# Seven-product output projections and two batches per attention output in a two-layer graph attention kernel

## The chip, the cores and the metric

The kernel runs on one core of one Trainium2 chip. The metric is device time in microseconds (us), from the first to the last instruction of the core. The engines are named as in the profile: PE is TensorE, PEld its weight loads, DVE is VectorE, ACT is ScalarE, POOL is GpSimd and SP is SyncE, which here issues all DMAs. Each engine works through its own queue in order, and waits on semaphores where it needs another's result.

## The reference

The input is `x` (128 batches, 128 nodes, 512 features, float32) with a boolean adjacency mask `adj` (128, 128, 128). Two layers follow, each `x = layernorm(x + attention(x, adj))`.

```python
# layer 0: 4 heads of 64
q, k, v = split_heads(x @ Wq), split_heads(x @ Wk), split_heads(x @ Wv)
attn = softmax(where(adj, q @ k.T * 64**-0.5, -max))
x = layernorm(x + (attn @ v) @ Wo + bo)
# layer 1: 8 heads of 64, norm in front, every node also sees itself
h = (x - mu) * rsqrt(var + 1e-5) * gamma + beta
q, k, v = split(h @ w_qkv.T)
attn = softmax(where(adj | eye, q @ k.T * 64**-0.5, -1e9))
x = layernorm(x + (attn @ v) @ w_out.T + b_out)
```

## The kernel before, in words

The batches are taken in 64 groups of two (G = 2). A software pipeline runs over steps s = 0 to 66 (`step`, L531). The order of the instructions on every engine is the order in which the Python code issues them, written out by hand under `manual_schedule` (L48). A step works on several groups at once: the layer-0 input products of group s, layer-0 attention of group s-1, layer-1 q and k products of group s-2, v products and layer-1 attention of group s-3. Within a step there are two halves, k = 2s and k = 2s+1, one for each batch of a group; `members(k)` (L381) names the layers and groups that take part.

- Input products: `product_0` (L337) for layer 0, `product` (L275) for layer 1. Both multiply in the Strassen-Winograd form: the two operands are cut into 2 x 2 blocks (batch by half of the contraction, half of the contraction by half of the output), and seven products of half size stand for eight. `sums` (L257) makes the four sums of the left blocks on POOL, `weight_sums` and `weight_sums_0` (L160, L175) those of the weights, once, on DVE. `INTO` (L272) says which PSUM bank takes each product and whether it starts or adds: 1, 6, 7 and 4 share bank "a", 5 and 3 bank "f", 2 has its own. After each product ACT or DVE takes the running value out, and the next product into the same bank waits for that.
- `scores` (L386): per head one product of q and k; then POOL fills a tile with the masked value (L410), DVE copies the unmasked scores over it (L412) and takes the row maximum (L415). For layer 1 the mask is first joined with the unit matrix (L407). The exponentials (`exps`, L421) run on ACT, head by head, and also give the row sums. `normalised` (L427) takes reciprocals on DVE and multiplies on POOL.
- `blocks` (L436) and `probs_arrive` (L454): DVE transposes 32 x 32 blocks, SP stores the result to memory and fetches it back with the blocks exchanged, which completes the transpose.
- `attend` (L458): values times probabilities for one batch k of each layer, then an ACT copy to SBUF (L474).
- `addend` (L476): the residual plus bias, on POOL; for layer 1 an ACT scaling first.
- `residual` (L487): the output product of one batch, one matmul of 128 x 512 for each 128 rows of the contraction (two for layer 0, four for layer 1, L493), then on DVE the addition of the residual (L499), the statistics (L501, L503), and on POOL the reciprocal roots (L506 to L517).
- `norms` (L522): subtract and multiply on DVE; called by `flush` (L56), which runs what `residual` put off. Layer 1's result is stored from there (L528), one batch at a time.
- `turn`, `arrive`, `in_order`, `finish` (L208, L219, L235, L245): the transpose of a layer's input: 32 x 32 blocks on DVE, a store and a fetch, then an ACT copy (layer 0) or ACT scaling with gamma and beta (layer 1), and `sums`.

The eight PSUM banks are split into five for the pool `ps_mm` and one each for "a", "f" and "a0"; layer 0's and layer 1's products share "f". The setup work, 12 row blocks of `w_qkv` and 4 of `w_out` transposed on PE, is spread over steps 0 and 1, a piece at a time (`p` in `step`, L532).

Of the kernel before, what the change touches and what calls it, by code (L numbers as in the profile page):

```python
# [27 lines left out]
def kernel(ctx: ExitStack, tc: tile.TileContext, x, adj, wq, wk, wv, wo, bo,  # L28
# [13 lines left out]
    four = ctx.enter_context(tc.tile_pool(name="four", bufs=4))  # L42
    dram = ctx.enter_context(tc.tile_pool(name="dram", bufs=2, space=bass.MemoryType.DRAM))
    ps_mm = ctx.enter_context(tc.tile_pool(name="ps_mm", bufs=5, space=PSUM))
# [9 lines left out]
    later, waiting = [], []  # L54

    def flush():  # L56
        while later:
            later.pop(0)()

    def exponentials(left=0):  # L60
        while len(waiting) > left:
            waiting.pop(0)()


    X, M = {}, {}

    def load(g):
        if g >= NG:
            return
        X[g] = four.tile([P, G, E], F32, tag="x", name=f"x_{g}")  # L70
        M[g] = four.tile([P, G, N], U8, tag="m", bufs=6, name=f"m_{g}")
        nc.sync.dma_start(X[g], x[g * G:(g + 1) * G].rearrange("b n e -> n b e"))
        nc.sync.dma_start(M[g], adj[g * G:(g + 1) * G].rearrange("b i j -> i b j"))
# [8 lines left out]
    mhalf = const.tile([P, 2], F32, name="mhalf")  # L82
# [6 lines left out]
    for i, w in enumerate((wq, wk, wv)):  # L89
        for h in range(2):  # L90
            nc.sync.dma_start(w0[:, :, h, i, :], w[:, h * HF:(h + 1) * HF].rearrange("(c p) f -> p c f", p=P))

    nc.scalar.activation(w0[:, :, :, 0, :], w0[:, :, :, 0, :], AF.Copy, scale=SCALE)
# [14 lines left out]

    spare = []
    for tag, n in (("qk1", 4), ("v1", 2), ("xT1", 2), ("xs1", 2)):  # L110
        rows_n = one.tile([P, n, E], F32, tag=tag, name=f"raw_{tag}")
        spare.extend(rows_n[:, i] for i in range(n))

    def load_transposed(dst, src, name, scaled=0):
        rows, cols = src.shape
        raws = []
        for r in range(rows // P):
            if not spare:
                raw = three.tile([P, cols], F32, tag="h", bufs=7, name=f"{name}_{r}")
            else:  # L120
                raw = spare.pop(0)
            nc.sync.dma_start(raw, src[r * P:(r + 1) * P, :])
            raws.append(raw)
# [36 lines left out]
    def weight_sums():  # L160
        for w, ws in ((w1qk, wsqk), (w1v, wsv)):
            for c in range(KH):
                if w is w1qk:
                    b11, b12 = w[:, c, :, 0], w[:, c, :, 1]
                    b21, b22 = w[:, KH + c, :, 0], w[:, KH + c, :, 1]
                else:
                    b11, b12 = w[:, c, 0], w[:, c, 1]
                    b21, b22 = w[:, KH + c, 0], w[:, KH + c, 1]
                t2, t3, t4 = ws[:, 0, c], ws[:, 1, c], ws[:, 2, c]
                nc.vector.tensor_sub(t3, b22, b12)  # L170
                nc.vector.tensor_sub(b12, b12, b11)
                nc.vector.tensor_sub(t2, b22, b12)
                nc.vector.tensor_sub(t4, b21, t2)

    def weight_sums_0():  # L175
        b11, b12, b21, b22 = (w0[:, c:c + KH, h].rearrange("p c t f -> p c (t f)")
                              for c in (0, KH) for h in range(2))
        t2, t3, t4 = (ws0[:, i].rearrange("p c t f -> p c (t f)") for i in range(3))
        nc.vector.tensor_sub(t3, b22, b12)
        nc.vector.tensor_sub(b12, b12, b11)  # L180
        nc.vector.tensor_sub(t2, b22, b12)
        nc.vector.tensor_sub(t4, b21, t2)

    weight_sums_0()
# [3 lines left out]
    setup.append(weight_sums)  # L188

    WO = (wo0, wo1)  # L190
    RATIO, H, XT, QK, V, QKV = {}, {}, {}, {}, {}, {}
# [14 lines left out]
    TURNED, SCR, RAW = {}, {}, {}  # L206

    def turn(l, g, b):  # L208
        if not 0 <= g < NG:
            return  # L210
        if b == 0:
            TURNED[l] = one.tile([P, 4, G * KC * 32], F32, tag=f"turned{l}", name=f"turned{l}_{g}")
        src = X[g][:, b] if l == 0 else H[g, b]
        nc.vector.transpose(TURNED[l].rearrange("p a (b c i) -> p a b c i", b=G, c=KC)[:, :, b],
                            src.rearrange("p (c a i) -> p a c i", a=4, i=32))
        if b == G - 1:
            SCR[l] = put(TURNED[l], f"scr{l}_{g}")

    def arrive(l, g):  # L219
        if not 0 <= g < NG:  # L220
            return
        RAW[l] = one.tile([P, 4, G, KC, 32], F32, tag=f"raw{l}", name=f"raw{l}_{g}")
        fetch(RAW[l].rearrange("p a b c i -> p a (b c i)"), SCR[l])

    def first_transposed():
        xT = XT[0, 0] = one.tile([P, KC, T], F32, tag="xT0", name="xT0_0")
        for b in range(G):
            pt = mm_tile(f"xt_{b}")
            for c in range(KC):
                nc.tensor.transpose(pt[:, c * N:(c + 1) * N], X[0][:, b, c * P:(c + 1) * P], ident)  # L230
            (nc.scalar.copy, nc.vector.tensor_copy)[b](xT[:, :, b * N:(b + 1) * N],
                                                       pt.rearrange("p (c n) -> p c n", c=KC))
        sums(0, 0)
# [11 lines left out]
    def finish(g):  # L245
# [4 lines left out]
        xT = XT[1, g] = one.tile([P, KC, T], F32, tag="xT1", name=f"xT1_{g}")  # L250
        for c in range(KC):
# [3 lines left out]
        sums(1, g)  # L255

    def sums(l, g):  # L257
        xT = XT[l, g]
        xs = one.tile([P, 4, KH, N], F32, tag=f"xs{l}", name=f"xs{l}_{g}")
        a = xT.rearrange("p (h c) (b n) -> p b h c n", h=2, b=2)  # L260
# [6 lines left out]
        XS[l, g] = xs  # L267
# [69 lines left out]
    def product_0(g, *which):  # L337
# [5 lines left out]
        for i in which:  # L343
# [10 lines left out]
            elif first:  # L354
                tag = {"a": "a0", "f": "f"}[bank]
                ACC[0, bank] = ps_st.tile([P, 512], F32, tag=tag, name=f"{bank}0_{g}")
# [11 lines left out]
            if i in (1, 5, 6):  # L368
                e = one.tile([P, 512], F32, tag=("e5_0" if i == 5 else f"e{i}"), name=f"e0_{i}_{g}")
                EV[0, i] = e[:, :3 * P]  # L370
# [8 lines left out]
    SM, SUM, PT, AT, XB = {}, {}, {}, {}, {}  # L379
# [6 lines left out]
    def scores(k):  # L386
        both = members(k)
        made = []
        for l, g, b in both:
# [11 lines left out]
            made.append(ps)  # L401
        for (l, g, b), ps in zip(both, made):
            K = HEADS[l] // 2
            mask = M[g][:, b, :]
            if l == 1:
                m1 = two.tile([P, N], U8, tag="m1", name=f"m1_{g}_{b}")
                nc.vector.tensor_tensor(m1, mask, eye, op=ALU.max)  # L407
                mask = m1
# [8 lines left out]
            SM[l, g, b], SUM[l, g, b] = sm, total  # L417
            waiting.append(lambda sm=sm, nmax=nmax, total=total, K=K: exps(sm, nmax, total, K))
        exponentials(1)

    def exps(sm, nmax, total, K):  # L421
# [14 lines left out]
    def blocks(k):  # L436
# [6 lines left out]
        t = one.tile([P, 4, sum(HEADS), 32], F32, tag="turned", name=f"turned_{k}")  # L443
        pT = one.tile([P, 4, sum(HEADS), 32], F32, tag="pT", name=f"pT_{k}")
        for l, g, b in both:
            lo, hi = slots[l]
            sm = SM.pop((l, g, b)).rearrange("p s k (q r) -> p q (s k) r", r=32)
            nc.vector.transpose(t[:, :, lo:hi, :], sm)  # L448
            PT[l, g, b] = pT[:, :, lo:hi, :]
        lo, hi = slots[both[0][0]][0], slots[both[-1][0]][1]  # L450
        t, pT = (u[:, :, lo:hi, :].rearrange("p a h i -> p a (h i)") for u in (t, pT))
        SCR["p"] = pT, put(t, f"scrp{hi - lo}_{k}")
# [5 lines left out]
    def attend(k):  # L458
        both = members(k)
        if not both:  # L460
            return
        for l, g, b in both:
            K = HEADS[l] // 2
            pT = PT.pop((l, g, b))
            pm = mm_tile(f"av{l}_{g}_{b}")

            for h in range(HEADS[l]):
                s, kk = h % 2, h // 2
                o = pm[s * D:(s + 1) * D, kk * N:(kk + 1) * N]
                v = QKV[g][:, b, kk, 2, s * D:(s + 1) * D] if l == 0 else V[1, g][:, b, h * D:(h + 1) * D]  # L470
                nc.tensor.matmul(o.rearrange("p (a r) -> p a r", r=32), v, pT[:, :, s * K + kk, :],  # L471
                                 start=True, stop=True)
            AT[l, g, b] = two.tile([P, INNER[l]], F32, tag=f"aT{l}", name=f"aT{l}_{g}_{b}")
            nc.scalar.copy(AT[l, g, b], pm[:, :INNER[l]])  # L474

    def addend(l, k):  # L476

        for _, g, b in [m for m in members(k) if m[0] == l]:
            if l == 0:
                xin = X[g][:, b, :]  # L480
            else:
                xin = H.pop((g, b))
                nc.scalar.activation(xin, xin, AF.Copy, scale=RATIO.pop((g, b)))  # L483
            nc.gpsimd.tensor_tensor(xin, xin, (bias0, bias1)[l], op=ALU.add)  # L484
            XB[l, g, b] = xin

    def residual(l, k):  # L487
        for _, g, b in [m for m in members(k) if m[0] == l]:
            aT = AT.pop((l, g, b))
            nk = INNER[l] // P  # L490
            pm = mm_tile(f"o{l}_{g}_{b}")
            for c in range(nk):
                nc.tensor.matmul(pm, aT[:, c * P:(c + 1) * P], WO[l][:, c, :],  # L493
                                 start=(c == 0), stop=(c == nk - 1))
            if l == 0:
# [134 lines left out]
```

## Time and profile before

| | us |
|---|---|
| median of three runs | 2984.34 |
| lowest, highest | 2983.19, 2987.64 |
| span of the profiled execution | 2982.7 |

| engine | busy us | instructions |
|---|---|---|
| PE | 2920.0 | 22089 |
| PEld | 2402.9 | 22089 |
| DVE | 1854.0 | 3291 |
| ACT | 1334.2 | 4619 |
| POOL | 1567.4 | 2055 |

Weight loads (PEld) overlap matmuls, so their time is not added to PE's. Groups of instructions that the change touches, from the list of groups: their line, count, and mean length of one.

| group | count | mean ns |
|---|---|---|
| L493 output product, 128x512 | 1536 | 600 |
| L499 addition of the residual, 128x512 | 256 | 672 to 692 |
| L524 norm of layer 1, of layer 0 | 128, 128 | 892, 547 |
| L335 addition, v products, 128x256 | 192 | 385 to 415 |
| L266 sums of left blocks, 128x256 | 512 | 726 to 731 |
| L474 attention copy, 128x256, 128x512 | 128, 128 | 357, 580 |
| L407 mask with unit matrix, 128x128 | 128 | 281 |

A mean length counts from the start of an instruction to its end; since matmuls are pipelined, the time that one adds is read from the starts of its neighbours in the timeline. One product of the source is two matmul instructions here.

### The profile page before, as it was taken

How to read it: one execution, taken by the hardware profiler on the slowest of the kernel's cores; microseconds unless marked ns; L12 is line 12 of the kernel's file. 1: busy time of each engine (PE TensorE's matmuls, PEld its weight loads, DVE VectorE, ACT ScalarE, POOL GpSimd, SP SyncE). 2: the span in 40 equal slices, each digit the busy share in tenths (PEclk: the TensorE clock that was granted, in tenths of full speed). 3: DMA queues.
4: the chain of work that ended last, by engine and by line, in shares of the span. 5: the costliest groups of instructions: out<-in, count | busy, mean ns of one | idle time of the engine just before them, and what ended most of it. 6: DMA issues, size and time to landing. Idle time of an engine off the chain costs nothing.

```text
span 2982.7 us, 59421 instructions
## 1 busy us (share of the span) xinstructions
PE 2920.0 (98%) x22089; PEld 2402.9 (81%) x22089; DVE 1854.0 (62%) x3291; ACT 1334.2 (45%) x4619; POOL 1567.4 (53%) x2055
## 2 busy tenths in 40 slices
PE   6899999999999999999999999999999999999997
PEld 5788888888888888888888888888888888888865
DVE  4466666666666666666656666666666666666654
ACT  2344444444444444444544444444444444444442
POOL 2455545545545555555555555455455455455543
PEclk8999999999999999999999999999999999999999
DMA  5454544544544544544544545545445445445332
GB/s 170 123 149 129 150 141 127 161 136 124 165 135 125 165 136 127 160 134 134 156 132 140 150 131 147 146 129 153 141 126 161 137 122 168 133 125 163 118 100 89
DMA packets 249136, 414.42 MB, mean 139 GB/s; under 512 B 41608, under 2 KB 181392, under 8 KB 248848
## 3 DMA queue, kind: packets, MB, share of 16 engines
q1 hardware_dynamic: 248848, 410.62, 46.3%
q8 instruction: 175, 2.87, 0.4%
q14 instruction: 113, 0.93, 0.1%
HBM read 209.72 MB, written 200.80 MB: 138 GB/s over the span
## 4 chain that ended last, share of the span: by engine, by line
PE 96%; DVE 1%; DMA 1%; ACT 1%; issue 0%; POOL 0%; SPq 0%; POOLq 0%; DVEq 0%; ACTq 0%
PE o L493 22%; PE qka L304 15%; PE a L361 12%; PE qkf L304 8%; PE va L304 8%; PE sc L400 6%; PE av L471 6%; PE f L361 6%; PE qkc L304 4%; PE vf L304 4%; PE c L361 3%; PE vc L304 2%; ACT sm L424 1%; DMA scrp<-turned 0%; DMA pT<-scrp 0%
## 5 line engine op out<-in xcount | busy, mean ns | idle before, releaser
L424 ACT ACTIVATE sm<-sm,nmax 128x128 f32<-128x128 f32 x1536 | 595.2, 389 | 618.6 <-DVE nmax L415 604.9
L493 PE MATMUL o<-wo,aT 128*128 128x512 f32 x1536 | 713.2, 600 | 10.0 <-ACT aT L474 10.0
L506 POOL TENSOR_SCALAR ve<-mv 128x1 f32<-128x1 f32 x256 | 57.0, 223 | 1133.0 <-DVE rec L432 798.8
L493 PEld LDWEIGHTS o<-wo,aT 128*128 128x128 f32 x1536 | 278.3, 191 | 269.3 <-issue 246.8
L433 POOL TENSOR_TENSOR sm<-sm,rec 128x512 f32<-128x512 f32 (+1 forms) x256 | 397.0, 1561 | 171.9 <-DVE rec L432 171.9
L412 DVE COPY_PREDICATED sm<-m,sc 128x512 f32<-128x512 uint8 (+1 forms) x512 | 271.0, 581 | 29.1 <-POOL sm L410 7.0
L424 ACT ACTIVATION_READ_ACCUMULATOR sm<-sm,nmax 128x1 f32 x1536 | 288.0, 187 | 0.0
L448 DVE STREAM_TRANSPOSE turned<-sm 128x512 f32<-128x512 f32 (+1 forms) x256 | 246.0, 965 | 45.0 <-POOL sm L433 45.0
L304 PE MATMUL qkf<-xs,w 128*128 128x128 f32 x2048 | 249.9, 275 | 0.1
L304 PE MATMUL qka<-xs,wsqk 128*128 128x128 f32 x2048 | 249.6, 275 | 0.0
L415 DVE TENSOR_REDUCE nmax<-sm 128x4 f32<-128x512 f32 (+1 forms) x256 | 244.0, 953 | 8.8
L304 PEld LDWEIGHTS qkf<-xs,w 128*128 128x128 f32 x2048 | 239.0, 192 | 0.6 <-POOL xs L266 0.4
L304 PEld LDWEIGHTS qka<-xs,wsqk 128*128 128x128 f32 x2048 | 239.0, 192 | 0.0
L524 DVE TENSOR_SCALAR h<-h,mv,rstd 128x512 f32<-128x512 f32 x128 | 70.0, 547 | 265.0 <-POOL rstd L513 265.0
L432 DVE RECIPROCAL rec<-total 128x4 f32<-128x4 f32 (+1 forms) x256 | 44.7, 175 | 296.6 <-ACT sm L424 296.6
L266 POOL TENSOR_TENSOR xs<-xT 128x256 f32<-128x256 f32 x256 | 186.0, 727 | 34.4 <-PE w_qkvt L129 14.5
L410 POOL MEMSET sm<- 128x512 f32 (+1 forms) x256 | 181.1, 735 | 1.4 <-DVE turned L448 1.3
L330 ACT COPY ev<-va 128x256 f32<-128x256 f32 x128 | 47.6, 372 | 298.7 <-PE va L304 298.7
L513 POOL TENSOR_TENSOR rstd<-ve,mhalf 128x2 f32<-128x2 f32 (+1 forms) x256 | 165.9, 648 | 21.3
L330 ACT COPY eqk<-qka 128x512 f32<-128x512 f32 x128 | 75.1, 587 | 214.4 <-PE qka L304 214.4
L484 POOL TENSOR_TENSOR h<-h,bias 128x512 f32<-128x512 f32 x128 | 162.7, 1271 | 7.0 <-ACT h L483 6.9
L484 POOL TENSOR_TENSOR x<-x,bias 128x512 f32<-128x512 f32 x128 | 162.2, 1267 | 0.0
(122 smaller groups left out, 5825.5 us busy)
## 6 DMA issues: line engine op xcount, KB each, us to landing
scrp<-turned SPq DMA_DIRECT2D x124, 768.0 KB, 3.3
pT<-scrp SPq DMA_DIRECT2D x496, 192.0 KB, 4.0
scr<-turned SPq DMA_DIRECT2D x127, 512.0 KB, 2.7
raw<-scr SPq DMA_DIRECT2D x508, 128.0 KB, 3.0
x<-in_x_dram SPq DMA_DIRECT2D x64, 512.0 KB, 4.2
out_dram<-y SPq DMA_DIRECT2D x128, 256.0 KB, 2.0
m<-in_adj_dram SPq DMA_DIRECT2D x64, 32.0 KB, 4.0
scrp<-turned SPq DMA_DIRECT2D x4, 512.0 KB, 3.2
```

The source lines that it names most:

```text
L266: nc.gpsimd.tensor_tensor(o, a0, a1, op=op)
L304: nc.tensor.matmul(o, lhsT, rhs, start=first and n == 0, stop=n == len(todo) - 1, skip_group_check=True)
L361: nc.tensor.matmul(acc[:, t * P:(t + 1) * P], lhsT, rhs, start=first and n == 0, stop=n == len(todo) - 1, skip_group_check=True)
L400: nc.tensor.matmul(ps[h % 2][:, h // 2, :], q_, k_, start=True, stop=True)
L410: nc.gpsimd.memset(sm, (NEG0, NEG1)[l])
L412: nc.vector.copy_predicated(sm[:, s], mask[:, None, :].to_broadcast([P, K, N]), ps[s][:, :K, :])
L415: nc.vector.tensor_reduce(nmax, sm, AX.X, ALU.max, negate=True)
L424: nc.scalar.activation(sm[:, s, k, :], sm[:, s, k, :], AF.Exp, bias=nmax[:, s, k:k + 1], accum_out=total[:, s, k:k + 1])
L433: nc.gpsimd.tensor_tensor(sm, sm, rec[:, :, :, None].to_broadcast([P, 2, K, N]), op=ALU.mult)
L448: nc.vector.transpose(t[:, :, lo:hi, :], sm)
L484: nc.gpsimd.tensor_tensor(xin, xin, (bias0, bias1)[l], op=ALU.add)
L493: nc.tensor.matmul(pm, aT[:, c * P:(c + 1) * P], WO[l][:, c, :], start=(c == 0), stop=(c == nk - 1))
```

## The change

It has these parts, cut to their core in the diff below.

1. The output products are formed in seven products too. `out_product` replaces the matmuls of `residual`: 128 x 256 outputs, one matmul per product for layer 0 and two for layer 1, and after every product DVE adds the bank straight into the residual, which lies in one tile `R[g]` for a group from load to store. `out_sums` makes the left sums on POOL, `weight_sums_out` the weights' sums once.
2. `attend` runs once per step, for both batches of a group; layer 0's two batches share one bank and one ACT copy. It takes the probabilities of the step before.
3. The norms run on ACT (Identity with scale and bias per row) instead of DVE, and layer 1's result is stored for two batches at once. `roots` works on both batches in one instruction, with two more small ones for the shift.
4. The layer-1 mask is made once per group (`with_self`). Masking and exponentials of the two layers are issued at separate places.
5. PSUM: four banks for `ps_mm`, and "a", "f", "a0", "f0". The probabilities' tile has two buffers; the input transposes of the two layers share one.
6. Start: `opening` replaces steps 0 and 1; group 1's input is transposed on PE as group 0's already was. The weights are loaded half by half.
7. End: the last batch's probabilities are transposed on PE (`blocks_direct`) and not through memory. Steps run from 2 to 67.
8. The order in `step` is written anew; `finish` is split in two halves; `load` is one group ahead and first in the step.

```diff
-    ps_mm = ctx.enter_context(tc.tile_pool(name="ps_mm", bufs=5, space=PSUM))
+    ps_mm = ctx.enter_context(tc.tile_pool(name="ps_mm", bufs=4, space=PSUM))
...
-    for i, w in enumerate((wq, wk, wv)):
-        for h in range(2):
+    for h in range(2):
+        for i, w in enumerate((wq, wk, wv)):
...
+    def out_product(l, g, *which):
...
+            for c in range(hk):
+                nc.tensor.matmul(acc, left[:, c], right[:, c], start=first and c == 0, stop=c == hk - 1,
+                                 skip_group_check=True)
+            b, h = {1: (0, 0), 2: (0, 0), 6: (0, 1), 3: (0, 1), 5: (1, 1), 7: (1, 1), 4: (1, 0)}[i]
+            part = R[g][:, b, h * EH:(h + 1) * EH]
+            nc.vector.tensor_add(part, acc, part)
...
+    def attend(s):
+
+        for l, g in ((0, s - 2), (1, s - 4)):
...
+        def norms():
+            for b in range(G):
+                nc.scalar.activation(R[g][:, b], R[g][:, b], AF.Identity, bias=shift[:, b:b + 1],
+                                     scale=root[:, b:b + 1])
+            if l == 1:
+                nc.sync.dma_start(out[g * G:(g + 1) * G].rearrange("b n e -> n b e"), R[g])
...
     def step(s):
...
+        load(s + 1)
+        made = scores(k)
+        masked(made, 0)
+        masked(made, 1)
+        exps(0, k)
+        addend(0, s - 2)
...
+        p("qk", s - 3, 4)
+        product_0(s, 1)
+        attend(s)
+        exps(1, k)
+        out_sums(0, s - 2)
+        product_0(s, 5, 2)
+        out_product(0, s - 2, 1, 5, 2)
+        if s < NG:
+            normalised(k)
+            addend(1, s - 4)
+        out_product(0, s - 2, 6)
+        product_0(s, 6)
+        if s < NG:
+            blocks(k, 0)
+        out_product(0, s - 2, 3, 7)
+        stats(0, s - 2, 0)
+        product_0(s, 3)
+        out_product(0, s - 2, 4)
+        stats(0, s - 2, 1)
+        product_0(s, 7)
+        p("v", s - 3, 1, 5)
...
+        blocks(k, 1)
+        p("v", s - 3, 2)
+        flush()
+        turn(1, s - 2)
+        arrive(1, s - 2)
+        probs_arrive(k)
+        k += 1
+        made = scores(k)
+        masked(made, 0)
+        p("v", s - 3, 6)
+        product_0(s, 4)
+        exps(0, k)
+        masked(made, 1)
+        exps(1, k)
+        p("v", s - 3, 3)
+        out_sums(1, s - 4)
+        flush(latest)
+        out_product(1, s - 4, 1, 5, 2)
+        p("v", s - 3, 7)
+        out_product(1, s - 4, 6, 3)
+        finish(s - 2, 0)
+        p("v", s - 3, 4)
+        normalised(k)
+        turn(0, s + 1)
+        finish(s - 2, 1)
+        out_product(1, s - 4, 7)
...
+        p("qk", s - 2, 1)
+        out_product(1, s - 4, 4)
+        stats(1, s - 4, 1)
+        p("qk", s - 2, 2, 5, 6)
+        in_order(s + 1)
         flush()
+        p("qk", s - 2, 3, 7)
-    for s in range(NG + 3):
+    opening()
+    for s in range(2, NG + 4):
         step(s)
```

## The prediction

> **What bounds the kernel now.** I read the page's busy times first, then busy time by stage, the chain that ended last, the costliest groups, and last the timeline of one step.
>
> ```profile
> PE 2920.0 (98%) x22089; PEld 2402.9 (81%) x22089; DVE 1854.0 (62%) x3291; ACT 1334.2 (45%) x4619; POOL 1567.4 (53%) x2055
> ```
> ```profile
> 0.00:50.00 50.00, 28.67 (x233) 27.28 (x233) 21.53 (x36) 14.25 (x30) 9.72 (x19) 0.99 0.71 226
> 50.00:100.00 50.00, 38.26 (x236) 31.76 (x237) 22.07 (x45) 13.57 (x43) 19.77 (x31) 0.81 0.31 94
> 100.00:150.00 50.00, 46.16 (x365) 39.78 (x364) 28.62 (x52) 21.35 (x78) 24.56 (x31) 0.97 0.40 117
> ...
> 1200.00:1500.00 300.00, 300.00 (x2275) 247.32 (x2274) 189.64 (x338) 137.31 (x473) 166.17 (x219) 1.00 0.49 145
> ...
> 2900.00:2950.00 50.00, 43.73 (x302) 33.83 (x301) 25.53 (x40) 20.27 (x71) 19.46 (x23) 0.97 0.25 80
> 2950.00:2983.00 33.00, 17.23 (x64) 8.82 (x64) 12.00 (x18) 5.85 (x21) 7.07 (x10) 0.86 0.27 87
> ```
> After the bounds of the stretch and its length come the busy times of PE, weight loads, DVE, ACT and POOL, the granted clock and DMA. The middle is one regime, PE busy without a gap; the first 150 us and the last 80 leave PE 37 and 22 us idle, and there its clock also falls. From 300 to 2850 us the list of PE's waits is empty. The chain says the same by line:
>
> ```profile
> PE o L493 22%; PE qka L304 15%; PE a L361 12%; PE qkf L304 8%; PE va L304 8%; PE sc L400 6%; PE av L471 6%; PE f L361 6%; PE qkc L304 4%; PE vf L304 4%; PE c L361 3%; PE vc L304 2%; ACT sm L424 1%; DMA scrp<-turned 0%; DMA pT<-scrp 0%
> ```
> So the time is a sum of matmuls. Scores of the first full step begin at 145.65 us in the chain, those of step 64 at 2854.6: 60 steps of **45.15 us**, a start of 145.65 and a tail of 128.1. PE's timeline of one step (start, length, the line) gives rates:
>
> ```profile
> 1324.56 1.95 PE L304 MATMUL qka<-xT,wsqk 128*128 128x128 f32 x16
> 1326.44 0.66 PE L471 MATMUL av<-pT,qkv 128*64 128x128 f32 x8
> ...
> 1334.84 1.88 PE L493 MATMUL o<-wo,aT 128*128 128x512 f32 x4
> 1336.55 1.03 PE L304 MATMUL va<-w,xT 128*128 128x256 f32 x4
> 1337.42 1.03 PE L304 MATMUL vf<-w,xs 128*128 128x256 f32 x4
> ```
> From start to start: four 512-column instructions take 1.71 us, 0.43 each; four of 256 columns 0.865, 0.216 each. A product in the source is two instructions.
>
> [...] this trace records 191 ns, still under the 216 ns of a 256-column matmul, so loads should stay hidden, as they do in the v rows. [...] qka above takes 1.88 us to av's start, 1.79 where a like product follows; leaving av costs about 0.1 again (1.00 against 0.90). [...] after 5.65 us idle at 44.5 us this trace grants 0.50 from 50 to 60.
>
> **The change part by part, per full step.**
> *Output products, PE.* Removed: 12 products of 512 columns, 24 x 0.43 = 10.32 us. Added: 7 for layer 0 and 14 for layer 1, of 256 columns, 42 x 0.216 = 9.07. **-1.25 us**, all on the path. Lower bound -1.32 (exact 7/8), upper +0.6 if each cost 0.26.
> *Attention of two batches.* One visit to the 64-column mode instead of two: -0.2 (0 to -0.2). [...] **Step: 43.8 us.**
> *DVE.* Added 14 additions 128x256 at 0.41 (v rows, L335): 5.74. Removed 4 of 512 (0.68 each, 2.73), norms 2 x 0.892 + 2 x 0.547 = 2.88, and one of two mask unions, 0.15 net. Sum 0: 28.7 of 43.8 us, beside PE.
> *ACT.* [...] one attention copy of 512 (0.58) for two of 256 (0.36): +3.1, to 23.8 us.
> *POOL.* Sums over attention outputs: 4 x 0.73 for layer 1, 4 x about 0.5 for layer 0 (between a fixed 0.2 and 0.73): +4.9. The small root operations: 5.1 before, between 4 and 6 after. 29.4 us of 43.8. All three hide below PE in throughput.
> *DMA.* Same bytes; one 512 KB store for two of 256, and the loads of x and mask move on SP's queue to the step's start, behind the store of the previous step. They have until the DVE turn some 30 us later; x landed in 4.2 us. Neither is on the path.
>
> **Waits.** Each engine runs in order, so I laid the new order out by hand from the durations above, step start = 0. ACT's exponentials are 0.385 us a head, start to start.
> - PE needs the attention copies at 10.5; ACT has layer 0's at about 7 and POOL its first sum at 7.5. Hidden.
> - Reciprocals stand in DVE's queue before the addition of output product 6. They wait for ACT's eight layer-1 exponentials, which stand behind three attention copies: 8.45 to 11.6. Reciprocals 12.6, addition 13.0, wanted by product 7 at 14.0. Slack 1.0.
> - v1 takes the bank of output product 4 at 17.6; that addition ends at 16.9, behind a 0.9 us stats pair. Slack 0.7.
> - Probabilities of the second batch: stored by 35.2 plus 3.3, fetched by 43 to 44; wanted at 48.5. Slack 4.
> - Layer 1's input is the tight one. Layer-0 stats end at 17.7, roots on POOL behind the 2.5 us bias addition 19.8, norms on ACT 21.1, DVE turns 22.0. Store: in the trace 512 KB land in 2.7 us, but a store at 1341.1 let SP fetch only at 1346.1, 5 us. So the fetch lands at 28.5 (median) to 31.8. ACT then makes half the input (1.1 us) and copies v4, and qk1 wants v4's bank at 31.85. A stall of 0 to 1.5 us. I take 0: in the new order only the 768 KB of probabilities go ahead of that store, and no 768 KB fetch.
> - qk1's later sums follow on POOL at 34.6, wanted at 36.3. Hidden.
>
> **The ends.** Start: before, PE does nothing between 6.7 and 15.25, because q's scaling precedes the transposed copies on ACT and a transpose of weights still in flight precedes the first product. Now product 1 needs only the scaled q and k, v; these land by about 9 to 10, with 1 us of scaling: **-5**. Sixteen weight subtractions (44.2 to 53.2 on DVE) stood before one batch's softmax; both batches of group 0 now pass before them, but group 1's scores wait behind them, with ACT blocked at those exponentials and PE idle some 7 us. The next layer-1 input costs another 9 of PE idle. Adding PE work of about 91 us (setup transposes, two groups' input products, steps 2 and 3) and 12 before the first product, 16 of these waits and 7 of slow clock and smaller waits gives **126** for the start of step 4, against 145.65; bounds 118 and 145.
> Tail: steps 64 and 65 lose their 9.4 us of input products: 36.5 and 36 with 2 us of waits each. The last softmax goes through PE transposes, without the two DMA trips of 4.0 and 3.2 us that stand in the chain at 2949.1 and 2954.5: half a step 8.5, then scores 0.7, mask 2.7, exponentials 3.1, normalise 2.4, transposes and copies 1.6, attention and copies 2.8, sum 0.8, seven products 6.5, stats, roots and norms 3.9, store 2.5, 2 more for hops: 37.5. Together **110**, against 128.1; bounds 102 and 122.
>
> Sum: 126 + 60 x 43.8 + 110 = 2864, against the profile's span of 2982.7; its three runs are 2983.2 to 2987.6, median 1.6 above the span. So **2866**.
>
> **The rivals.**
> 1. *Late layer-1 input.* The wait at qk1 takes the place of the saved matmuls. For it: 5 us for that store in the trace. Against: the store has another neighbour now. At 1.2 us of stall: 2866 + 72 = **2938**.
> 2. *The ends give nothing* (126 and 110 become 145 and 128): **2903**. For it: [...] three long DVE, DMA chains remain in the start.
> 3. *Slower: DVE's queue stops PE.* Mechanism: the reciprocals ahead of output product 6. Slack 1.0 us; every us that ACT's exponentials end later than 11.6 then goes one for one into the step. It decides from 1.0 + 1.35 (the step's gain) + 0.6 (37 us of the ends over 60 steps) = 3 us late. At 3.5 late, 2.5 lost: **3016**. For it: ACT has three copies and, from the last step, norms ahead of them. Against: in the trace these exponentials end 10.4 us after the step's start already.
> 4. *The product doesn't do what it says:* 256-column matmuls with a new load each at 0.26 us instead of 0.216: 42 x 0.26 = 10.9, step +1.8, **2974**. Against: the v rows hold 0.216 with just such loads.
>
> **How the numbers follow.** Forecast 0.58, rival 1 0.17, rival 2 0.14, rival 3 0.08, rival 4 0.03. The forecast's own bounds are about 2835 to 2895; taking in rival 2 and most of rival 1 the range is 2835 to 2940, which leaves out rivals 3 and 4 and the worse part of rival 1, with 3 in 100 below. A measurement tells about 0.2% (6 us) from no change: faster 0.90, within 0.02 (part of rival 4), slower 0.08.
>
> **What would show it.** The output products' chain share falls from 22% to about 20.3% of a shorter span, 9.07 us a step; full steps 43.8 us apart; PE's waits in the middle still empty. Rival 1 shows as PE waiting at a qk start for ACT, rival 3 as PE waiting for DVE at an output product or v1, rival 2 as the first full step after 140 us. I am wrong if steps exceed 44.5 us, or if PE gains a repeated wait.

## The result, and the profile after

The changed kernel took **2955.76 us**, the median of four runs (2953.34 to 2958.32), against 2983.77 before (2981.52 to 2987.64): a ratio of 0.9905, 95% interval 0.9888 to 0.9922. It is faster, by 1% where 4% was forecast, and it lies 16 us above the top of the range. Its profiled execution spans 2956.5 us. The page first: busy times, and the chain by line (the chain is the work that ended last, followed back from the last instruction: at each step to what it had waited for).

```profile
PE 2854.8 (97%) x23257; PEld 2631.1 (89%) x23257; DVE 1818.2 (61%) x3618; ACT 1515.5 (51%) x4811; POOL 1752.2 (59%) x2439
...
PE qka L305 17%; PE a L361 11%; PE oa L397 10%; PE qkf L305 8%; PE va L305 8%; PE sc L425 7%; PE f L361 6%; PE av L529 6%; PE of L397 6%; PE qkc L305 4%; PE vf L305 4%; PE c L361 3%; PE oc L397 3%; ACT xT L252 2%; PE vc L305 2%
```

Output products (oa, of, oc at L397) now hold 10 + 6 + 3 = 19% by the rounded shares, near the 20.3% that was foretold. New at the end of the line is an ACT entry with 2%, where before only PE lines came to more than 1%. PE's busy time fell by 65 us and the span by only 26, so PE now waits. Its list of waits (what waited for what: us in total, times, the longest) gives the place:

```profile
PE qka L305 <- ACT v L333: 40.0, 63, 3.1
PE qka L305 <- ACT xT L252: 9.6, 1, 9.6
PE oa L397 <- ACT aT L534: 7.0, 1, 7.0
```

The first line is the repeated wait, 63 times some 0.63 us on average (0.57 in most steps); the other two stand once each, in the start. Busy time by stage (bounds, length, PE, weight loads, DVE, ACT, POOL, granted clock, DMA):

```profile
50.00:100.00 50.00, 29.60 (x209) 27.39 (x210) 29.68 (x51) 11.84 (x33) 16.05 (x25) 0.80 0.33 96
...
1200.00:1500.00 300.00, 295.97 (x2455) 274.17 (x2454) 186.09 (x375) 158.53 (x503) 183.38 (x252) 1.00 0.50 143
```

The middle, without a gap before, is 4 us short in 300, 0.6 a step. From 50 to 100 us PE does less than before (38.26 then). In PE's timeline step 4's first scores begin at 146.19 and step 64's at 2820.38, which splits the missed time in three:

| | forecast | after |
|---|---|---|
| start, to step 4 | 126 | 146.2 |
| 60 steps | 60 x 43.8 = 2628 | 60 x 44.57 = 2674.2 |
| tail, from step 64 | 110 | 136.1 |
| span | 2864 | 2956.5 |

Half of the miss, 46 us, is the repeated wait with the slower product behind it; the chain shows what it is (start, length, piece).

```profile
1335.00 0.86 PE of L397 x4
1335.86 0.88 PE va L305 x4
1336.74 0.02 issue
1336.77 1.09 ACT xT L252 x2
1337.86 0.27 ACT v L333
1338.12 0.04 issue
1338.16 2.05 PE qka L305 x16
```

ACT does not begin layer 1's new input (`xT`, L252) when the fetch lands but when PE ends the v product of L305. That product is v4 (product 4 of the seven v products) of the *previous* group, and it reads the previous input, from the same tile. ACT's write has to wait for the tile's last reader. In the program `finish(s - 2, 0)` stands ahead of `p("v", s - 3, 4)`, so the copy of v4 (L333) stands in ACT's queue behind the writes that wait for v4. The first qk product (qk1) wants both: its half of the input, and the bank that the copy frees. Nothing but 0.86 us of PE work (output product 7) lies between.

### The profile page after: what moved, and what is told of

It reads as the page before. It is cut to its first block, busy times and chain, and to the rows that moved or that the text cites. A ratio compares the mean times of both kernels' runs of the same rounds, so it can differ in the third digit from the quotient of the medians.

```text
span 2956.5 us, 63007 instructions
## 1 busy us (share of the span) xinstructions
PE 2854.8 (97%) x23257; PEld 2631.1 (89%) x23257; DVE 1818.2 (61%) x3618; ACT 1515.5 (51%) x4811; POOL 1752.2 (59%) x2439
## 4 chain that ended last, share of the span: by engine, by line
PE 93%; ACT 3%; DVE 1%; POOL 1%; issue 1%; DMA 1%; SPq 0%; ACTq 0%; POOLq 0%; DVEq 0%
PE qka L305 17%; PE a L361 11%; PE oa L397 10%; PE qkf L305 8%; PE va L305 8%; PE sc L425 7%; PE f L361 6%; PE av L529 6%; PE of L397 6%; PE qkc L305 4%; PE vf L305 4%; PE c L361 3%; PE oc L397 3%; ACT xT L252 2%; PE vc L305 2%
## 5 line engine op out<-in xcount | busy, mean ns | idle before, releaser
L550 POOL TENSOR_TENSOR r<-r,bias 128x1024 f32<-128x1024 f32 x128 | 303.0, 2367 | 2.9 <-ACT r L549 2.9
L401 DVE TENSOR_TENSOR r<-oa,r 128x256 f32<-128x256 f32 x512 | 215.7, 421 | 80.6 <-PE oa L397 79.8
L305 PE MATMUL qkf<-xs,w 128*128 128x128 f32 x2048 | 249.6, 275 | 0.0
L305 PE MATMUL qka<-xs,wsqk 128*128 128x128 f32 x2048 | 249.6, 275 | 0.0
L305 PEld LDWEIGHTS qka<-xs,wsqk 128*128 128x128 f32 x2048 | 239.0, 192 | 0.0
L305 PEld LDWEIGHTS qkf<-xs,w 128*128 128x128 f32 x2048 | 239.0, 192 | 0.0
L336 DVE TENSOR_TENSOR qk<-qkf,eqk 128x512 f32<-128x512 f32 x64 | 44.3, 692 | 298.8 <-PE qkf L305 275.5
L268 POOL TENSOR_TENSOR so<-aT 128x128 f32<-128x128 f32 (+1 forms) x256 | 151.9, 593 | 113.8 <-ACT aT L534 113.8
L397 PE MATMUL of<-wo,so 128*128 128x256 f32 x768 | 210.3, 383 | 5.3 <-POOL so L268 5.3
L397 PE MATMUL oa<-wso,so 128*128 128x256 f32 x768 | 213.1, 386 | 0.5 <-DVE r L401 0.5
L595 ACT ACTIVATE r<-r,shift,root 128x512 f32<-128x512 f32 x256 | 194.3, 807 | 22.7 <-POOL shift L584 22.7
L252 ACT ACTIVATE xT<-raw,gb 128x256 f32<-128x256 f32 x256 | 139.7, 594 | 117.3 <-PE va L305 111.7
L375 DVE TENSOR_TENSOR qkv<-c,e 128x384 f32<-128x384 f32 x64 | 35.7, 557 | 254.4 <-PE c L361 252.5
L305 PEld LDWEIGHTS qka<-xT,w 128*128 128x128 f32 x1024 | 122.7, 196 | 75.0 <-ACT v L333 65.3
```

The lines of the kernel that those rows point to most:

```text
L268: nc.gpsimd.tensor_tensor(o, a0, a1, op=op)
L305: nc.tensor.matmul(o, lhsT, rhs, start=first and n == 0, stop=n == len(todo) - 1, skip_group_check=True)
L397: nc.tensor.matmul(acc, left[:, c], right[:, c], start=first and c == 0, stop=c == hk - 1, skip_group_check=True)
L401: nc.vector.tensor_add(part, acc, part)
L550: nc.gpsimd.tensor_tensor(R[g], R[g], (bias0, bias1)[l][:, None, :].to_broadcast([P, G, E]), op=ALU.add)
```

## The experiments

Ratios are to runs of the kernel before on the same chip.

**The repeated wait.** Two edits remove it, if the reading is right. One issues v4 earlier and the input later:

```diff
-        out_product(1, s - 4, 6, 3)
-        finish(s - 2, 0)
+        out_product(1, s - 4, 6)
         p("v", s - 3, 4)
+        out_product(1, s - 4, 3)
+        finish(s - 2, 0)
```

> The product v4 is issued one output product earlier, so that 1.7 us of matmuls and not 0.86 lie between it and qk1. Theory W (the write of layer 1's input waits for v4, its buffer's last reader, and v4's copy stands behind it on ACT): PE's 63 waits of 0.57 us at qk1 vanish, full steps 43.8 us instead of 44.57, time about 2908 to 2912. Theory R (the fetched input lands late): the wait stays or moves, time within 5 us of 2956.

Measured: 2909.39 us, ratio 0.9743 [0.9729, 0.9758], with full steps of 43.71 us (43.80 on average over the 60). The other leaves the order alone and gives each half of the input a tile of its own; v4 reads only the second half, so the first needn't wait for it:

```diff
-            XT[1, g] = one.tile([P, KC, T], F32, tag="xT1", name=f"xT1_{g}")
...
+        xT = one.tile([P, KH, T], F32, tag=("xT1", "xT1h")[half], name=f"xT1_{g}_{half}")
```

> Layer 1's transposed input lies in two tiles, one for each half of the contraction; nothing else moves. Theory W: the first half then waits only for earlier readers, ACT starts it when the fetch has landed, some 1.5 us before v4 ends, and the wait at qk1 vanishes: steps about 43.8 us, time about 2910. Theory R: ACT starts it at the same time as now, no change, 2956.

Measured: 2907.74, 0.9741 [0.9726, 0.9755]. Its chain at the same place:

```profile
1360.15 0.86 PE va L311 x4
1361.01 0.86 PE oa L403 x4
1361.88 1.78 PE qka L311 x16
```

ACT is gone from it, PE goes from v4 through output product 7 into the qk product, and that takes 1.78 us instead of 2.05. No transfer was moved, so the wait was for the old tile and not for late data. Wait (0.57 a step) and slow product (0.27) are nearly all of the 0.86 us by which the steps of 43.71 are shorter. In ACT's timeline of this run the first half of the input now starts when the fetch lands, at 1359.83, and is made by 1360.92; the copy of v4 ends at 1361.42. With the old tile out of the way the transfer is next, and by these times it has about half a us to spare.

A third edit exchanges only the two lines, v4 ahead of `finish(s - 2, 0)`, so that the copy stands first in ACT's queue:

```diff
-        finish(s - 2, 0)
         p("v", s - 3, 4)
+        finish(s - 2, 0)
```

> v4 is issued ahead of the first half of layer 1's input, so ACT copies v4 first. If only the copy's place in ACT's queue made the wait (theory C), it shrinks from 0.57 us to about 0, time about 2912. Theory W: qk1 then waits for the input instead, which still starts after v4: no change within 5 us of 2956.

Measured: 2941.42, 0.9854 [0.9839, 0.9868]; both numbers missed. A step takes 44.35. Its chain at the place:

```profile
1329.43 0.61 ACT xT L252
1330.04 0.04 issue
1330.09 0.49 PE qka L305 x2
1330.57 0.00 issue
1330.57 1.83 PE qka L305 x14
```

The copy is out of the way, and the qk product starts after the first of ACT's two input instructions instead of after both and the copy; then it runs 0.49 + 1.83 = 2.32 us instead of 1.78, its second matmul being held until the second instruction ends. The step gains 0.22 us of the 0.86. So the copy's place is a minor part, the reuse of the tile the major.

**Are seven products worth 1.25 us?** Plain products of 512 columns were put back, all else as changed; the left sums on POOL and the sums of the weights are left out.

```diff
+            if i in (1, 3):
+                b, bank = {1: (0, "a"), 3: (1, "f")}[i]
...
+                    nc.tensor.matmul(acc, aT[:, b, c], w[:, c, :], start=c == 0, stop=c == 2 * hk - 1)
+                nc.vector.tensor_add(R[g][:, b], acc, R[g][:, b])
+            continue
```

> The output products are plain again: 512 columns, one bank and one DVE addition for each batch; the left sums on POOL and the weights' sums for them are left out. Seven products worth 1.25 us a step on PE: steps 45.8 us, time about 3025 to 3035 if the wait at qk1 stays; about 2990 if that wait shrinks to nothing because ACT and DVE are freer. If the seven products are worth nothing on the chip (weight loads bound): 2956 or less.

Measured: 3075.02, 1.0302 [1.0285, 1.0319], far from all numbers: the wait at the qk product grew from 40.0 to 94.3 us, as the products that stood beside it had moved. With the input in halves as well:

> xT1_halves with the plain output products of out_plain (left sums and weight sums for them left out). With the wait at qk1 gone from both, the difference to xT1_halves is the seven products alone. Theory of the prediction (1.25 us of matmul time a step): about 2908 + 75 to 85 = 2983 to 2993. If out_plain's extra 119 us belonged to the products themselves: about 3025.

Measured: 3021.8, 1.0115 [1.01, 1.013], again with that wait, 34.8 us over 63. Last with the two plain products at the places of products 1 and 7, so that one stands ahead of qk1:

> As plain_halves, but the second plain output product is issued at the place of product 7 and not of 3, so that 3.4 us of matmuls lie between v4 and qk1, and qk1 no longer waits. The seven products alone are then the difference to xT1_halves. Theory (1.25 us of matmul time a step): 2908 + 75 to 85 = 2983 to 2993. If the products cost more than their matmuls: above 3005.

Measured: 3017.96, 1.0107 [1.0093, 1.0121], with steps of 45.7 us against 43.8 in `xT1_halves`. Its list of waits has a new first line:

```profile
PE va L312 <- DVE v L343: 37.8, 64, 2.9
```

In the chain of one step its output products take 10.30 us, those of `xT1_halves`, with seven, 9.12: the matmuls save **1.18 us**, close to the forecast's 1.25. Another 0.59 us a step (37.8 / 64) is that wait, in which a v product waits for DVE to empty its bank, and some 0.27 us is that v product running longer behind it (1.13 us instead of 0.86). `xT1_halves` has no such repeated wait: in this order the small output products also fill that time. Each of the three plain kernels kept a repeated wait, so none gives the worth of seven products by its total time; the 1.18 us is read from the chains.

**The v product before the second scores.** In the changed kernel the second half's scores take 1.74 us instead of 1.54, which I put down to a bank that DVE frees late, behind transposes. The second v product was moved ahead of those, on top of `xT1_halves`:

```diff
-        blocks(k, 1)
         p("v", s - 3, 2)
+        blocks(k, 1)
```

> xT1_halves, with product v2 issued ahead of the layer-1 transposes, so that its DVE addition, which frees the bank of the second scores, does not stand behind 1.25 us of transposes. Theory (the scores of each second half take 1.74 us in the chain and not 1.54 for that reason): 0.2 us a step, 2895 to 2898 against 2908. Rival (v2's matmuls end too late in any case): within 2 us of 2908.

Measured: 2965.93, 0.9937 [0.9925, 0.995]; I had expected nothing like it. The scores did take 1.55 us. But the chain of a step now runs through memory:

```profile
1377.44 1.55 PE sc L431 x21
1378.99 0.06 issue
1379.05 1.26 DVE turned L212 x2
1380.31 0.03 DVE sm L449
1380.34 4.70 DMA scr<-turned
...
1386.36 3.73 DMA raw<-scr
...
1390.12 1.09 ACT xT L251 x2
1391.21 0.26 ACT v L339
```

DVE makes the turned layer-1 input after the scores instead of beside them, because its transposes now stand in the queue behind v2's addition, for which DVE is idle 2.1 us. The store is issued 2.9 us after the scores begin (1.8 in `xT1_halves`), only 1.2 us behind the 768 KB store of probabilities (2.6 there), and lands late: the median of all 512 KB stores of a transposed input is 3.8 us, against 2.7. The fetch then comes too late, and the qk product waits 50.8 us over 58. This is rival 1's mechanism, brought about by an edit that exchanges two lines. The delay, 1.1 us of later issue and about 1 us of slower landing, is more than the half us that the transfer had to spare in `xT1_halves`.

**The start.** PE's first output product waits 7.0 us for the attention copy, behind DVE's weight subtractions. Those of layer 1 were moved into steps 2 and 3:

```diff
-        weight_sums(w1qk, wsqk)
-        weight_sums(w1v, wsv)
-        weight_sums_out(1)
...
+        if s == 2:
+            weight_sums(w1qk, wsqk)
```

> The weight subtractions of layer 1 leave the start and go behind group 1's masking: those for q and k behind the second masking of step 2, those for v to the end of step 2, those for the output product to the end of step 3. Theory (they block DVE, so ACT and PE, from 50.5 to 66 us): the 7 us wait at the first output product vanishes with the slow clock behind it, time 2946 +- 3. Rival (the start is bound by the chain through layer 1's first input, which only moves with what feeds it, or the subtractions delay the next probabilities instead): within 3 us of 2956.

Measured: 2953.75, 0.9885 [0.987, 0.99]. The 7.0 us shrank to 1.2, but step 4 begins only 4.2 us earlier (142.0): a wait of 2.3 us for DVE appears at an attention product. Three kernels below that have the changed kernel's start (`end_early`, `end_memory`, `last_step`) begin step 4 between 144.4 and 145.2, so 2 to 4 us were gained where about 10 were expected.

**The tail.** Three edits. The total times of `end_early` and `last_step`, like that of `sums_later`, have intervals that overlap the changed kernel's, so a gain of 2 to 4 us is not clear of noise; what moved is read from the traces. First the probabilities ahead of the output products, as in the full steps, instead of behind them (`normalised(k)`, `addend(1, s - 4)` and `blocks(k, 0)` at their early places for all steps below NG + 3):

> The order that holds up to step 63 (reciprocals, residual and layer-0 transposes ahead of output product 6) also holds for steps 64 to 66. Theory (the late normalise makes POOL and DVE late for the scores of step 64 and for v2): PE's 3.3 us wait there vanishes, time 2948 to 2952. Rival (without input products between them, reciprocals ahead of product 6 stop the output products until the exponentials are done): 3 to 8 us slower than 2956.

2953.09, 0.9886 [0.9869, 0.9902]. The scores' wait of 3.3 us is gone, and output product 7 waits up to 2.0 us instead, for the addition of product 6, which stands behind the reciprocals in DVE's queue; rival 3's mechanism, in the tail. The last softmax through memory again, as before (`blocks(k, 0, 1)` instead of `blocks_direct(k)`):

> The last batch's probabilities go through memory as all others. Theory (store and fetch take about 3.5 + 1.7 + 3.1 us against about 2 us of PE transposes and copies): 5 to 7 us slower, 2961 to 2963. Rival (the last step waits for POOL's residual and sums anyway): within 2 us of 2956.

2957.13, 0.99 [0.9886, 0.9915]: no change, although PE now waits 7.8 us for those DMA trips. Transposing on PE was worth nothing in this order: without the trips, the chain of the last step runs through ACT and POOL just as long. And the last step's attention copy ahead of the norms, the last residual scaled and biased a step earlier:

```diff
-        if s == NG + 3:
-            addend(1, s - 4)
...
+            if s == NG + 2:
+                addend(1, s - 3)
...
-        flush()
+        if s != NG + 2:
+            flush()
```

> Only the last two steps change: the residual of the last group's layer 1 is made in step 66, and group 62's norms and store wait until the attention copies of step 67 are issued. Theory (in the last step ACT's copies stand behind norms that wait for POOL's roots, and POOL's sums behind the residual: PE waits 4.46 + 0.57 us and its clock halves after): 5 to 9 us faster than 2956. Rival (the last softmax or its transposes end just as late): within 2 us.

2951.53, 0.9884 [0.987, 0.9897]: 4 us by the medians. The spans lie 8.6 apart, but the changed kernel's profiled execution is the slowest of its four; tails with that kernel's code take from 131.1 us (`sums_later`) to its own 136.1, this one 129.0.

**All together.** First with the move of v2:

> xT1_halves, v2_halves, sums_later and end_early together. If the gains add (48, 0 to 12, 2 to 9 and 3 to 6 us): 2885 to 2903.

2968.91, 0.9939 [0.9926, 0.9953], slower than the halves alone. Then without it, and with and without `end_early`:

> The changed kernel with layer 1's turned input in two tiles (xT1_halves, 2907.7), the weight sums in the other order (sums_later), the end's scores first (end_early) and the last step's attention copy ahead of its norms (last_step). Theory A, the gains of start and tail lie in other stretches than the steps' and add: 2907.7 less 2 to 4 for the start, less 2 for end_early, less 4 to 8 for the last step: 2893 to 2901, the steps at 43.7 us. Theory B, start and tail are bound by something common (granted clock after idle time, GpSimd's queue) and what one wait gives back another takes: 2903 to 2908. Theory C, the loss of combo_all was not the move of the second v product but the other edits together with the halves: above 2920, with steps of 44.2 or more.

> As all_but_v2, without end_early: the end keeps the changed kernel's order. Theory A: 2895 to 2903, some 2 us above all_but_v2. Theory B: 2903 to 2908, no difference between the two. Theory D, end_early's wait of output product 6 for the reciprocals costs what its scores gain: this kernel is the faster of the two by 1 to 3 us.

Measured: 2900.72 (0.972 [0.9706, 0.9733]) and 2900.66 (0.9722 [0.9709, 0.9735]). So it was the move that cost `combo_all` its gain; `last_step` is the only other difference. Start and tail add 7 us to `xT1_halves` by the medians, 6 by the ratios, whose intervals just overlap. Both times lie within theory A's ranges, but the two kernels don't differ, as theory B had it: `end_early` adds nothing. Both beat the changed kernel by 55 us. `halves_ends` has a start of 141.2, steps of 43.80 (141.23 to 2769.45), and a tail of 129.9; `all_but_v2`, with the same code in the start, begins step 4 at 143.6.

**Subtractions beside GpSimd.** In the start of the changed kernel DVE's 20 weight subtractions last from 50.5 to 66.0. Some of 256 columns take twice and one six times as long as before (0.42):

```profile
56.49 0.42 DVE L169 TENSOR_TENSOR w<-w 128x256 f32<-128x256 f32 x1
56.95 0.84 DVE L170 TENSOR_TENSOR wsv<-w 128x256 f32<-128x256 f32 x1
...
60.42 0.42 DVE L170 TENSOR_TENSOR wsv<-w 128x256 f32<-128x256 f32 x1
60.88 2.46 DVE L171 TENSOR_TENSOR wsv<-w,wsv 128x256 f32<-128x256 f32 x1
```

POOL's timeline of the same stretch:

```profile
57.58 0.79 POOL L268 TENSOR_TENSOR xs<-xs,xT 128x256 f32<-128x256 f32 x1
...
60.05 0.52 POOL L441 MEMSET sm<- 128x512 f32 x1
60.53 2.53 POOL L550 TENSOR_TENSOR r<-r,bias 128x1024 f32<-128x1024 f32 x1
```

That one bias addition (one of 64, not of 32) was taken away, so this kernel leaves the bias out for the first group:

```diff
-        addend(0, s - 2)
+        if s > 2:
+            addend(0, s - 2)
```

> The changed kernel without the first of its 32 bias additions of layer 0 on GpSimd (one 128x1024 TENSOR_TENSOR of 2.5 us for group 0, left out). Theory P, VectorE's subtraction beside it is held up by GpSimd's instruction: the subtraction that took 2.46 us beside it takes 0.42 like its neighbours, VectorE's subtractions end some 2 us earlier, and the first output product of step 2 follows some 2 us earlier; the ones beside the four left sums stay at 0.83. Theory N, the long subtraction waits for something else (its own operands, a DMA): it stays above 2 us.

DVE's timeline, and then PE's (in brackets the idle time before and what ended it):

```profile
60.90 0.43 DVE L171 TENSOR_TENSOR wsv<-w,wsv 128x256 f32<-128x256 f32 x1
```
```profile
68.17 1.22 PE L397 MATMUL oa<-wo,aT 128*128 128x256 f32 x2 [4.84 <-ACT aT L534]
```

The subtraction takes 0.43 us, the subtractions end 2.0 us earlier (64.0), and beside the four sums they keep 0.83 to 0.99: theory P. The second half of the theory isn't shown: the first output product starts at 68.17 instead of 70.18, after a wait of 4.84 us instead of 7.03, but `last_step` and `end_early`, with the addition in place, wait 4.7 and 4.9 us there. This kernel ran once (2952.4 us), and its total decides nothing.

## Why the prediction missed, step by step

- **Output products, -1.25 us a step: right.** 1.18 in the chain; 256-column matmuls hold 0.216, so rival 4 is out.
- **One attention visit: right in sum.** One visit of 2.77 us; without the repeated wait the whole step is 43.80 on average, forecast 43.8. The 0.1 us by which that forecast lies above 45.15 - 1.25 - 0.2 was an allowance of mine; no run tests it.
- **DVE, ACT, POOL and DMA hidden: right in throughput.** A step of the middle has 27.6 us of DVE, 23.6 of ACT and 27.2 of POOL (the 300 us line above, for 44.57 us), where 28.7, 23.8 and 29.4 were forecast; a norm on ACT takes 0.807 us, and one of POOL's left sums over layer 0's attention output 0.455, put at about 0.5. The norm's length within ACT's 23.8 was my own estimate; the kernel before has no such instruction. The DMA engines are busy 50%.
- **"Layer 1's input is the tight one ... A stall of 0 to 1.5 us. I take 0": this step failed, for 46 us.** The wait is at that place and within its bounds (0.86 us with the slow product); I chose their lower end. But what I weighed there was the transfer, and it was not at fault. The sequence "ACT then makes half the input and copies v4, and qk1 wants v4's bank" named each piece and left out one relation: the input goes into a tile whose last reader is v4. I had followed data from writer to reader, and never a buffer from its last reader to its next writer. Rival 1 named the waiting instruction, at 1.2 us a step, and was wrong about the cause here; its sign, PE waiting at a qk start for ACT, can't tell a late fetch from a tile still in use. That its cause can come is shown by `v2_halves`.
- **The start, 126: the term "7 of slow clock and smaller waits" was too small.** The first product began at 11.6, forecast 12. The two long waits, put at "some 7 us" and "another 9", came to 7.0 and 9.6; that the first fits is luck, for kernels with the same code up to there wait between 4.7 (`last_step`) and 9.6 (`v4_early`). PE's time before step 4 was put at 91 us of work; the stretch shows 107 us busy at a mean granted clock (the share of PE's full clock) of 0.89:

```profile
0.00:146.26 146.26, 107.03 (x795) 99.05 (x795) 73.12 (x132) 48.15 (x141) 48.09 (x76) 0.89 0.47 142
```

  The 91 was not undersized: at the rates of a full step (0.112 us for 128 columns, 0.216 for 256, 0.064 for a score matmul) the matmuls of this stretch come to about 89 us, an estimate from their counts. So 16 of the 20 missed us are the same work taking longer, at a lower clock or held by an operand, which the traces don't separate, and the rest is more idle time. The term of 7 came to 27 (146.2 less 91, 11.6 and 16.6). The subtractions took 15.5 us, where the sixteen that were counted took 9 before; the four new ones add 2.8. Of the 3.7 that remain, 2.0 went with one GpSimd addition (`no_bias`); the four subtractions beside GpSimd's sums, 3.44 us together, took 1.7 before.
- **The tail, 110: two terms failed.** "36.5 and 36 with 2 us of waits each" came to 43.8 and 41.0: scores wait 3.3 us, and what follows runs slow (four 256-column matmuls 1.71 to 2.00 us instead of 0.86). Some of that is this one execution: `no_bias` and `sums_later` have the same code there and tails of 131.2 and 131.1, 5 us less of the 26 missed. And the last sum, 37.5 for the last two steps, has "seven products 6.5, stats, roots and norms 3.9" once. The chain goes through them twice, 51.3 us from 2905.21 on; here the first round and what it hands on (in a part of the chain):

```profile
2926.41 0.42 DVE r L401
2927.03 1.91 POOL sm L468
...
2931.43 0.71 DVE st L561
2932.70 0.72 POOL root L571
2933.77 0.23 POOL shift L584
...
2934.75 0.80 ACT r L595
2935.55 1.23 ACT r L549 x2
2936.85 2.35 POOL r L550
2939.20 0.70 POOL so L268
```

  Norms of step 66, scaling and bias for step 67, and only then the last left sums. The trips through memory, which I counted as 7 us gained, gave nothing (`end_memory`).
- **Rival 2, the ends give nothing: it came, and its sign too.** Step 4 began after 140 us. Start and tail took 282.3 us, before 273.8, so in this execution the ends even cost 8.5. **Rival 3** did not come in the full steps.
- **The test that I named held:** steps beyond 44.5 us and a repeated wait of PE are both there.

What stays open: of the 35 us by which `halves_ends` still exceeds the forecast, all in start and tail, no single wait beyond those forecast was found that holds more than 5.3. That they come from granted clock and GpSimd's queue together is argued, not shown.

## What to carry to other kernels

When work is reordered, follow each single-buffered tile from its last reader to its next writer, along every queue between, as carefully as data from writer to reader; a reader that is issued *after* the new writer's data are ready is a wait, and a second tile for half the data can be all it needs. Where a step's slack is put at "0 to 1.5 us" and the step runs 60 times, the choice of 0 is the forecast, and 1.5 belongs in the range with a real chance. At the ends, where engines wait for one another, sum the chain round by round, and don't price stretches with long waits at the full clock: this start was granted 0.89 of it on average, the tail 0.90.

## What the runs showed of the hardware

One VectorE subtraction of 256 columns took 2.46 us beside a GpSimd bias addition of 2.53 us, and 0.43 once that addition was gone (`no_bias`). The four beside GpSimd's left sums took 0.83 to 0.94 us in the changed kernel; the same four took 0.42 to 0.43 before, in a stretch (44 to 54 us) in which POOL had nothing to do. I had priced the subtractions from that stretch.

PE's slow clock after a wait shows in its products: from the start of the qk product after the 9.6 us wait to that of the next one are 3.37 us (granted clock 0.50 from 90 to 94), and 1.78 for the same product in a full step (`xT1_halves`). How slow the products are differs between executions of the same code: after the 3.3 us wait of the tail the fourteen score matmuls took 2.07 us in the changed kernel, where the granted clock of the next 7 us was 0.54, and 1.16 in `sums_later`. A 512 KB store of a transposed input landed in a median of 2.7 us in `xT1_halves` and 3.8 in `v2_halves`, with the same bytes and, in the step read above, the larger store ahead of it nearer by 1.4 us.
